# An expert layer on one Trainium2 core: token slots in parts of 64, two experts side by side in a block

## The chip, the core and the metric

The kernel runs on one core of a Trainium2 chip. The core has five engines, each with its own queue of instructions: TensorE (PE; matrix products and transposes, with weight loads shown apart as PEld), VectorE (DVE), ScalarE (ACT), GpSimd (POOL) and SyncE (SP, which here only issues transfers). Sixteen DMA engines move data between the chip's main memory (HBM) and the on-chip memory SBUF; TensorE writes its results into PSUM. The metric is the device time of one execution, in microseconds (us).

## What is computed

The program is one block of a graph network: two graph attention layers and a linear attention over 1250 tokens of 768 features, then a layer of eight experts. The change is in the expert layer alone. Cut to that, the reference is:

```python
def _L0_ffn_ref(x, router_w, w_gate, w_up, w_down, ws_gate, ws_up, ws_down, sg_w, sg_b):
    probs = softmax(x @ router_w)                      # 1250 x 8
    gates, idx = top_k(probs, 2)
    gates = gates / sum(gates)
    dense_g = sum(one_hot(idx, 8) * gates[..., None], axis=-2)
    g = silu(einsum('bsd,edh->bseh', x, w_gate))       # 8 experts, 768 x 768 each
    u = einsum('bsd,edh->bseh', x, w_up)
    expert_out = einsum('bseh,ehd->bsed', g * u, w_down)
    routed = einsum('bse,bsed->bsd', dense_g, expert_out)
    shared = silu(x @ ws_gate) * (x @ ws_up) @ ws_down
    alpha = sigmoid(x @ sg_w + sg_b)
    return alpha * shared + (1 - alpha) * routed
```

Every token goes to two experts, so there are 2500 pairs of token and expert. All numbers are f32.

## The kernel before

Everything up to line 697 (the graph and attention layers) is left alone by the change. The expert layer has four stages.

**Routing (lines 725 to 852).** Tokens are normalised, written to HBM (`xd`) and transposed; the router's scores follow. VectorE then finds the two experts of each token (`hot`), counts the tokens of each expert (`seen`), and lays the experts out one after another in a list of slots. An expert gets as many blocks of 128 slots as its tokens need: `cmp` compares its count with 0, 128, 256, ... (`steps`), `nb` is its number of blocks, `sb` the running sum over the experts. `slot` says in which slot each pair lies; POOL scatters the token numbers into the list `who` in HBM, and SP loads it back as `ids`. `blk` holds the expert of each block (`be`: how many experts end at or before it, from `jb` and `sb`), and in its last column the number of blocks.

**Shared expert (lines 855 to 867).** A dense layer of width 384 on TensorE; routing runs beside it on the other engines. Its weights `wsgu` and its input `xfT` share SBUF with what comes later: pool `wb` (line 870) takes memory that this stage gives back at `sh.close()`, pool `wa` (line 714) has its own and can be filled while the stage runs.

**Expert blocks (lines 872 to 963).** A block is 128 slots of one expert. For each block, POOL gathers the rows of its tokens (`xin`, line 895), TensorE transposes them (`rows`, to `xT`), multiplies with the gate and the up weights (`up`, half of the 768 columns at a time), ScalarE and VectorE make silu(gate) times up (`h`), TensorE transposes that (`hidden`, to `hT`) and multiplies with the down weights (`down`), and the result is written to `ys` in HBM. Three weight tiles of 2304 KB are fetched for each block by SP (`fetch`), at an address that depends on the block's expert; even blocks use the tiles of pool `wa`, odd blocks those of `wb`.

The number of blocks depends on the data. `NSURE` (23) blocks always run, in a pipeline written out by hand: within step j, TensorE does the first half of up(j), the transposes of block j-1's hidden rows, the second half of up(j), the transposes of block j+1's rows, and down(j-1). Gate and up weights of block j+2 are fetched as soon as up(j) has read the tiles, down's of j+1 when down(j-1) has. Blocks beyond 23, up to `NBLK` (27), stand in nested conditions (line 956) and run one step after another.

**Combination (lines 965 to 987).** POOL gathers each token's two rows of `ys` (20 gathers `yg`), TensorE makes the shared expert's last product (`pds`), VectorE adds everything with its factors, and SP and ACT write the output.

A helper's line stands for all its uses: 906 and 907 are the transposes and their copies out of PSUM, 920 the gate and up products, 929 the down products, 901 the weight fetches.

Of the kernel before, what the change touches and what calls it, by code (L numbers as in the profile page):

```python
# [8 lines left out]
F32 = mybir.dt.float32  # L9
# [4 lines left out]
I32 = mybir.dt.int32  # L14
# [5 lines left out]
P = 128  # L20
# [20 lines left out]
NSURE = -(-2 * N // P) + NE // 2 - 1  # L41
NBLK = (2 * N + NE * (P - 1)) // P
# [15 lines left out]
def gps_block(ctx: ExitStack, tc: tile.TileContext, x, src, dst, norm_g, norm_b, W1, a_src1, a_dst1, b1,  # L58
# [643 lines left out]

    fp = ctx.enter_context(tc.tile_pool(name="ffn", bufs=1, reuse_waits="tile"))
# [4 lines left out]
    blk = fp.tile([TP, NBLK + 1], I32, name="blk")  # L708
    ids = fp.tile([P, NBLK], I32, name="ids")
# [4 lines left out]
    wa = ctx.enter_context(tc.tile_pool(name="wa", bufs=1, reuse_waits="tile"))  # L714

# [9 lines left out]
    with tc.tile_pool(name="fln", bufs=2, reuse_waits="tile") as pw, tc.tile_pool(name="flnps", bufs=1, space=PSUM, reuse_waits="tile") as ps:  # L725
# [9 lines left out]
        steps = pw.tile([TP, NE, NT], F32, name="steps", bufs=1)  # L735
        nc.gpsimd.iota(steps, pattern=[[0, NE], [P, NT]], base=0, channel_multiplier=0,
                       allow_small_or_imprecise_dtypes=True)
        jb = pw.tile([TP, NBLK, NE], F32, name="jb", bufs=1)
        nc.gpsimd.iota(jb, pattern=[[1, NBLK], [0, NE]], base=0, channel_multiplier=0,
# [62 lines left out]
        cmp = pw.tile([TP, NE, NT], F32, name="cmp", bufs=1)  # L802
        nc.vector.tensor_tensor(cmp, seen[:, NT, :, None].to_broadcast([TP, NE, NT]), steps, ALU.is_gt)
        nb = pw.tile([TP, NE], F32, name="nb", bufs=1)
        nc.vector.tensor_reduce(nb, cmp, axis=AX.X, op=ALU.add)
        sb = pw.tile([TP, NE + 1], F32, name="sb", bufs=1)
# [4 lines left out]
        nc.vector.scalar_tensor_tensor(first, sb[:, None, 0:NE].to_broadcast(S3), float(P), seen[:, 0:NT, :],  # L811
# [24 lines left out]
        ends = pw.tile([TP, NBLK, NE], F32, name="ends", bufs=1)  # L836
        nc.vector.tensor_tensor(ends, jb, sb[:, None, 1:NE + 1].to_broadcast([TP, NBLK, NE]), ALU.is_ge)
        be = pw.tile([TP, NBLK + 1], F32, name="be", bufs=1)
        nc.vector.tensor_reduce(be[:, 0:NBLK], ends, axis=AX.X, op=ALU.add)
        nc.vector.tensor_scalar(be[:, 0:NBLK], be[:, 0:NBLK], float(NE - 1), None, op0=ALU.min)  # L840
        nc.vector.tensor_copy(be[:, NBLK:NBLK + 1], sb[:, NE:NE + 1])
        nc.vector.tensor_copy(blk, be)

# [28 lines left out]
    with tc.tile_pool(name="fps", bufs=1, space=PSUM, reuse_waits="tile") as ps:  # L872
        n_blk = nc.values_load(blk[0:1, NBLK:NBLK + 1], min_val=0, max_val=NBLK)

        two = range(2)
        ws = [[(wa, wb)[i].tile([P, KD, D], F32, name=f"w{n}{i}") for n in "gud"] for i in two]
# [10 lines left out]
        experts = {}  # L887

        def fetch(j, *parts):

            if j >= NBLK:
                return
            if 0 in parts:
                experts[j] = nc.sync.value_load(blk[0:1, j:j + 1], min_val=0, max_val=NE - 1)
                nc.gpsimd.indirect_dma_start(
                    out=xin[j % 2], out_offset=None, in_=xd,
                    in_offset=bass.IndirectOffsetOnAxis(ap=ids[:, j:j + 1], axis=0),
                    bounds_check=N - 1, oob_is_err=False)
            for p in parts:
                w = (w_gate, w_up, w_down)[p]  # L900
                nc.sync.dma_start(ws[j % 2][p], w[bass.ds(experts[j], 1)].rearrange("o (k p) f -> p (o k) f", p=P))
# [12 lines left out]

        def up(j, s):
            xT, h = xTs[j % 2], hs[j % 2]
            half = slice(s * HALF, (s + 1) * HALF)
            for pt, w in ((pgs[s], ws[j % 2][0]), (pus[s], ws[j % 2][1])):
                for k in range(KD):
                    nc.tensor.matmul(pt[:, :HALF], xT[:, k, :], w[:, k, half], start=(k == 0), stop=(k == KD - 1))  # L920
            nc.scalar.activation(h[:, half], pgs[s][:, :HALF], AF.Sigmoid)  # L921
            nc.vector.tensor_mul(h[:, half], h[:, half], pgs[s][:, :HALF])  # L922
# [92 lines left out]
```

## Time and profile before

| what | us |
|---|---|
| median of 3 runs | 1679.14 (1664.4 to 1679.84) |
| the profiled execution | 1679.8 |
| its span, first to last instruction | 1678.1 |
| before the shared expert and routing, 0 to 896 | 896 |
| routing and shared expert, 896 to 1028.6 | 132.6 |
| 23 blocks of the pipeline, 1028.6 to 1585.7, but for the last one's down | 557.1 |
| that down and the conditional block, 1585.7 to 1622.0 | 36.3 |
| combination, 1622.0 to the end | 56 |

The view of busy slices cuts the span into 40 equal parts, one digit for each: 9 means that the engine was busy 90% of it or more. The view of stretches gives, for a stretch of time, each engine's busy time and number of instructions, then the granted TensorE clock (1.00 is full speed), the share of time that the DMA engines were busy, and GB/s. In the list of groups, a line shows the source line, the engine, what is written from what, shapes, how often, then busy time and the mean duration of one in ns, and the idle time of the engine before them with what ended it. The timeline shows start, length in us, engine, line and how many instructions were merged into the row. An f32 product leaves two records of TensorE, so a block's 36 products are 72 records. Ends of TensorE's records are modelled; their starts are what to read.

### The profile page before, as it was taken

The numbers are of one execution on the slowest core, as the hardware profiler recorded it, in microseconds if no ns is written. First come the engines' busy times: TensorE is split into PE (matmuls) and PEld (weight loads), VectorE is DVE, ScalarE is ACT, GpSimd is POOL, SyncE is SP. The second block draws the span as 40 slices with busy tenths as digits, with TensorE's granted clock in tenths as the row PEclk, the third lists the DMA queues.
The fourth block names the chain that finished last, engine by engine and source line by source line (L and its number), as shares of the span: only waits on it lengthen the run. The fifth ranks groups of instructions, "written<-read, shape, count | busy, mean of one in ns | idle before, by whom it ended". The sixth has DMA issues, their size and how long they took to land. (4 is left out here: it accounts for less than half of the span.)

```text
span 1678.1 us, 15224 instructions
## 1 busy us (share of the span) xinstructions
PE 1587.1 (95%) x5769; PEld 985.6 (59%) x5769; DVE 728.0 (43%) x1342; ACT 369.9 (22%) x635; POOL 142.6 (9%) x175
## 2 busy tenths in 40 slices
PE   6899889999999899999988999999999999999996
PEld 5666544444455599965555855666666666666553
DVE  7888459212443499966787221111111111111116
ACT  3122211111000188830672200101111110111000
POOL 2211000000000000010000051000000000000014
PEclk9999899999999999999997699999999999999998
DMA  7200041002111100021012267988889888888668
GB/s 193 74 1 1 2 139 53 1 0 68 38 38 38 48 31 31 31 73 27 20 44 84 65 114 251 365 324 333 314 304 355 306 309 332 327 313 305 240 225 247
DMA packets 110020, 254.35 MB, mean 152 GB/s; under 512 B 16019, under 2 KB 38676, under 8 KB 109940
## 3 DMA queue, kind: packets, MB, share of 16 engines
q1 hardware_dynamic: 89578, 206.59, 34.4%
q0 software_dynamic: 14704, 36.62, 7.4%
q10 hardware_dynamic: 5658, 10.08, 1.7%
q8 instruction: 50, 0.82, 0.2%
q14 instruction: 30, 0.25, 0.1%
HBM read 234.39 MB, written 18.80 MB: 151 GB/s over the span
## 5 line engine op out<-in xcount | busy, mean ns | idle before, releaser
L920 PE MATMUL pgb<-wg,xT 128*128 128x384 f32 x576 | 194.0, 487 | 2.3 <-ACT xT L907 2.3
L920 PE MATMUL pub<-wu,xT 128*128 128x384 f32 x576 | 193.6, 486 | 0.0
L929 PE MATMUL pdb<-wd,hT 128*128 128x384 f32 x576 | 189.8, 486 | 0.4 <-ACT hT L907 0.4
L532 PE MATMUL pp<-wkv,xnT 128*125 128x512 f32 x360 | 161.6, 598 | 0.1
L920 PEld LDWEIGHTS pub<-wu,xT 128*128 128x128 f32 x576 | 109.4, 190 | 76.3
L614 PE MATMUL pa<-G,u 125*125 125x199 f32 x800 | 140.4, 336 | 11.1 <-DVE h L622 6.0
L920 PEld LDWEIGHTS pgb<-wg,xT 128*128 128x128 f32 x576 | 107.5, 190 | 72.7 <-ACT xT L907 3.0
L929 PEld LDWEIGHTS pdb<-wd,hT 128*128 128x128 f32 x576 | 107.6, 190 | 70.9 <-ACT hT L907 0.7
L614 PEld LDWEIGHTS pa<-G,u 125*125 125x125 f32 x800 | 135.6, 190 | 16.2 <-issue 7.2
L922 DVE TENSOR_TENSOR h<-h,pgb 128x384 f32<-128x384 f32 x48 | 26.6, 554 | 194.8 <-ACT h L921 194.8
L532 PEld LDWEIGHTS pp<-wkv,xnT 128*125 128x125 f32 x360 | 65.9, 190 | 73.7 <-issue 73.3
L931 DVE COPY y<-pdb 128x768 f32<-128x768 f32 x24 | 23.0, 958 | 188.4 <-PE pdb L929 188.4
L411 PE MATMUL ph<-wg,xnT 128*125 128x400 f32 x240 | 101.9, 531 | 2.6 <-PEq L425 2.5
L595 DVE TENSOR_TENSOR ea<-ea,eb 125x625 f32<-125x625 f32 x120 | 93.9, 804 | 14.8 <-ACT eb L594 7.6
L597 DVE SCALAR_TENSOR_TENSOR u<-ea,cntT 125x625 f32<-125x625 f32 x120 | 94.0, 804 | 14.1 <-PE pa L614 8.0
L594 ACT ACTIVATE eb<-r,g_ss 125x625 f32<-125x625 f32 x120 | 95.0, 816 | 20.7 <-DVE ea L595 20.6
L921 ACT ACTIVATE h<-pgb 128x384 f32<-128x384 f32 x48 | 23.5, 490 | 329.6 <-PE pgb L920 329.6
L479 DVE CUSTOM_DVE_ANT_0 junk<-ssb,absent 125x1250 bf16<-125x1250 f32 x60 | 87.7, 1462 | 15.1 <-DMA ssb<-g_srow_d 13.9
L562 PE MATMUL pq<-xnT,wq 128*128 128x500 f32 (+1 forms) x216 | 81.2, 520 | 4.2 <-DMA wq<-in_L_mix_w_qkv_dram 3.7
L923 DVE TENSOR_TENSOR h<-h,pub 128x384 f32<-128x384 f32 x48 | 26.6, 554 | 134.1 <-PE pub L920 134.1
L648 PE MATMUL pu<-wu,xnT 128*125 128x384 f32 x240 | 81.4, 489 | 2.5 <-DVE acc L653 2.5
L575 PE MATMUL pu<-wp,at 128*125 128x384 f32 x240 | 80.5, 488 | 1.4 <-DVE acc L578 1.1
(234 smaller groups left out, 1762.9 us busy)
## 6 DMA issues: line engine op xcount, KB each, us to landing
wg<-in_L_ffn_w_gate_dram SPq DMA_DIRECT2D x25, 2304.0 KB, 8.9
wu<-in_L_ffn_w_up_dram SPq DMA_DIRECT2D x25, 2304.0 KB, 28.7
wd<-in_L_ffn_w_down_dram SPq DMA_DIRECT2D x25, 2304.0 KB
ys<-y ACTq DMA_DIRECT2D x24, 384.0 KB, 7.1
r<-g_rrow_d POOLq DMA_DIRECT2D x12, 610.4 KB, 8.1
wq<-in_L_mix_w_qkv_dram SPq DMA_DIRECT2D x18, 384.0 KB, 3.4
wkv<-in_L_mix_w_qkv_dram SPq DMA_DIRECT2D x6, 768.0 KB
acc<-in_x_dram POOLq DMA_DIRECT2D x10, 375.0 KB, 10.8
```

The source lines that it names most:

```text
L411: nc.tensor.matmul(ph[:, :2 * CG], xnT[:, k, tok], wg[:, k, s * 2 * CG:(s + 1) * 2 * CG], start=(k == 0), stop=(k == KD - 1))
L479: nc.vector.tensor_tensor_reduce(out=junk, in0=self.ssb, in1=absent[:, dt, :], scale=1.0, scalar=-3.0e38, op0=ALU.add, op1=ALU.max, accum_ ...
L532: nc.tensor.matmul(pp, xnT[:, k, tok], wkv[:, k, :, :], start=(k == 0), stop=(k == KD - 1))
L562: nc.tensor.matmul(pq[:, :qw], wq[:, k, :], xnT[:, k, tok], start=(k == 0), stop=(k == KD - 1))
L575: nc.tensor.matmul(pu[:, s, :HALF], at[:, k, i * TP:(i + 1) * TP], wp[:, k, s * HALF:(s + 1) * HALF], start=(k == 0), stop=(k == KD - 1))
L594: nc.scalar.activation(eb, r[:, 1, :], AF.Exp, bias=ss02[:, st, h:h + 1])
L595: nc.vector.tensor_max(ea, ea, eb)
L597: nc.vector.scalar_tensor_tensor(u, ea, 1.0, cntT[:, st, half * W:(half + 1) * W], op0=ALU.min, op1=ALU.mult)
L614: nc.tensor.matmul(pa[i][:, :CO + 1], u[:, i * TP:(i + 1) * TP], G[:, st, h, :CO + 1], start=(st == 0), stop=(st == NT - 1))
L648: nc.tensor.matmul(pu[:, :HALF], xnT[:, k, t * TP:(t + 1) * TP], wus[s][:, k, :], start=(k == 0), stop=(k == KD - 1))
L920: nc.tensor.matmul(pt[:, :HALF], xT[:, k, :], w[:, k, half], start=(k == 0), stop=(k == KD - 1))
L929: nc.tensor.matmul(pd[:, s, :HALF], hT[:, k, :], ws[j % 2][2][:, k, s * HALF:(s + 1) * HALF], start=(k == 0), stop=(k == KD - 1))
```

## The change

Slots are laid out in parts of 64 instead of blocks of 128 (`PART`, `NPART` = 2), and every expert gets at least two parts. A block is still 128 slots, two parts, but each part has its own expert. With the same inputs `NSURE` becomes 22 and `NBLK` 26.

The weights are kept in three rings of two slots (`wg`, `wu`, `wd`). Block j fetches the weights of its second part's expert into slot j % 2. Its first part belongs to the same expert or to the one whose weights block j-1 fetched, and so lies in the one slot or the other: `place` (computed on VectorE, 0 or 1) says in which, and TensorE reads it into a register (`places`). Each product over 128 slots is now two over 64 (`product`): the first part's results go to PSUM partitions 0 to 63, with weights at an address from the register, the second part's to 64 to 127. The two alternate for each of the six pieces of the sum.

Because block j may still read the slot that block j-1 filled, block j+1's weights can only be fetched when block j has read its own: gate's after all of gate(j), up's after up(j), down's after down(j). For this `up` is parted into `gate` and `up`, both halves of gate now come before up, and the row gathers (`gather`) stand apart from the weight fetches. The gate and up rings lie in pool `wa`, down's in `wb`.

```diff
-NSURE = -(-2 * N // P) + NE // 2 - 1
-NBLK = (2 * N + NE * (P - 1)) // P
+PART = 64
+NPART = P // PART
+NBLK = -(-((NE - 2) * NPART - 2 * (-N // PART)) // NPART)
+NSURE = -(-(2 * N + NE * PART // 2) // P)
...
+    place = fp.tile([TP, NBLK, NPART], I32, name="place")
...
+    rings = [wa.tile([P, 2, KD, D], F32, name=f"w{n}") for n in "gu"]
...
-        steps = pw.tile([TP, NE, NT], F32, name="steps", bufs=1)
+        steps = pw.tile([TP, NE, -(-N // PART)], F32, name="steps", bufs=1)
...
         nc.vector.tensor_reduce(nb, cmp, axis=AX.X, op=ALU.add)
+        nc.vector.tensor_scalar(nb, nb, float(NPART), None, op0=ALU.max)
...
-        ends = pw.tile([TP, NBLK, NE], F32, name="ends", bufs=1)
-        nc.vector.tensor_tensor(ends, jb, sb[:, None, 1:NE + 1].to_broadcast([TP, NBLK, NE]), ALU.is_ge)
+        ends = pw.tile([TP, NBLK * NPART, NE], F32, name="ends", bufs=1)
+        nc.vector.tensor_tensor(ends, jb, sb[:, None, 1:NE + 1].to_broadcast([TP, NBLK * NPART, NE]), ALU.is_ge)
+        pe = pw.tile([TP, NBLK, NPART], F32, name="pe", bufs=1)
+        nc.vector.tensor_reduce(pe, ends.rearrange("p (b i) e -> p b i e", i=NPART), axis=AX.X, op=ALU.add)
+        nc.vector.tensor_scalar(pe, pe, float(NE - 1), None, op0=ALU.min)
         be = pw.tile([TP, NBLK + 1], F32, name="be", bufs=1)
-        nc.vector.tensor_reduce(be[:, 0:NBLK], ends, axis=AX.X, op=ALU.add)
-        nc.vector.tensor_scalar(be[:, 0:NBLK], be[:, 0:NBLK], float(NE - 1), None, op0=ALU.min)
+        nc.vector.tensor_copy(be[:, 0:NBLK], pe[:, :, NPART - 1])
         nc.vector.tensor_copy(be[:, NBLK:NBLK + 1], sb[:, NE:NE + 1])
         nc.vector.tensor_copy(blk, be)
+        nc.vector.tensor_tensor(pe, pe, be[:, 0:NBLK, None].to_broadcast([TP, NBLK, NPART]), ALU.is_equal)
+        nc.vector.tensor_tensor(pe, pe, odd.rearrange("p b i -> p (b i)")[:, 0:NBLK, None].to_broadcast([TP, NBLK, NPART]),
+                                ALU.is_equal)
+        nc.vector.tensor_copy(place, pe)
...
-        ws = [[(wa, wb)[i].tile([P, KD, D], F32, name=f"w{n}{i}") for n in "gud"] for i in two]
+        rings.append(wb.tile([P, 2, KD, D], F32, name="wd"))
...
+        def fetch(j, i):
+            if j >= NBLK:
+                return
+            if i == 0:
+                experts[j] = nc.sync.value_load(blk[0:1, j:j + 1], min_val=0, max_val=NE - 1)
+            w = (w_gate, w_up, w_down)[i]
+            nc.sync.dma_start(rings[i][:, j % 2], w[bass.ds(experts[j], 1)].rearrange("o (k p) f -> p (o k) f", p=P))
+
+        def places(j):
+            at = [j % 2] * NPART
+            if j > 0:
+                for i in range(NPART - 1):
+                    at[i] = nc.tensor.value_load(place[0:1, j, i:i + 1], min_val=0, max_val=1)
+            spots[j] = at
+
+        def product(j, i, pt, rows, s):
+            for k in range(KD):
+                for q, at in enumerate(spots[j]):
+                    part = slice(q * PART, (q + 1) * PART)
+                    w = rings[i][:, at] if isinstance(at, int) else rings[i][:, bass.ds(at, 1)].rearrange(
+                        "p o k f -> p (o k) f")
+                    nc.tensor.matmul(pt[part, :HALF], rows[:, k, part], w[:, k, s * HALF:(s + 1) * HALF],
+                                     start=(k == 0), stop=(k == KD - 1))
...
-        fetch(0, 0, 1, 2)
-        fetch(1, 0, 1, 2)
+        for j in two:
+            gather(j)
+            for i in range(2):
+                fetch(j, i)
+            if j == 0:
+                fetch(j, 2)
+        places(0)
         rows(0)
         for j in range(NSURE):
-            up(j, 0)
+            gate(j, 0)
             if j > 0:
                 hidden(j - 1)
-            up(j, 1)
-            if j + 2 < NSURE + 1:
-                fetch(j + 2, 0, 1)
+            gate(j, 1)
+            if j > 0 and j + 1 < NSURE + 1:
+                fetch(j + 1, 0)
+            if j + 1 < NSURE:
+                places(j + 1)
+            for s in two:
+                up(j, s)
+            if j > 0 and j + 1 < NSURE + 1:
+                fetch(j + 1, 1)
+            gather(j + 2) if j + 2 < NSURE + 1 else None
             if j + 1 < NSURE:
                 rows(j + 1)
             if j > 0:
                 down(j - 1)
-                if j + 1 < NSURE + 1:
-                    fetch(j + 1, 2)
+                fetch(j, 2)
         hidden(NSURE - 1)
         down(NSURE - 1)
+        fetch(NSURE, 2)
```

`gate` is the first third of the old `up` (the gate products, sigmoid, and the product with silu's input), the new `up` the rest; the conditional blocks change in the same way and test the number of parts.

## The prediction

> **What bounds the kernel now.** I read the page's busy slices first, then the busy time by stretch, the groups of instructions, and the timeline. In the slices, and in the stretch from 1028.60 us (the first expert block) to 1585.70 (the end of the pipelined blocks), TensorE is busy almost without a break: 556.50 of 557.10 us, at full granted clock. The DMA engines are busy 84% of it, so they have a margin, but not a large one.
>
> ```profile
> PE   6899889999999899999988999999999999999996
> ...
> DMA  7200041002111100021012267988889888888668
> ```
> ```profile
> 1028.60:1585.70 557.10, 556.50 (x1904) 337.55 (x1903) 71.77 (x114) 61.30 (x136) 22.93 (x23) 1.00 0.84 320
> ```
>
> The groups say what fills it: the three expert products. One f32 product of 128x384 leaves two records here.
>
> ```profile
> L920 PE MATMUL pgb<-wg,xT 128*128 128x384 f32 x576 | 194.0, 487 | 2.3 <-ACT xT L907 2.3
> ...
> L929 PE MATMUL pdb<-wd,hT 128*128 128x384 f32 x576 | 189.8, 486 | 0.4 <-ACT hT L907 0.4
> ```
>
> The timeline of one block shows the price of a record (start to start, 12 records from 1079.50 to 1083.37: 322.5 ns) and of a block (1071.10 to 1095.64: 24.54 us). No gap is left: waits of the other engines end inside it, and only the number of TensorE records and their spacing count.
>
> ```profile
> 1071.10 4.03 PE L920 MATMUL pgb<-wg,xT 128*128 128x384 f32 x12
> 1074.97 4.03 PE L920 MATMUL pub<-wu,xT 128*128 128x384 f32 x12
> 1078.84 0.82 PE L906 MATMUL ptr<-ident,h 128*128 128x128 f32 x6
> 1079.50 4.04 PE L920 MATMUL pgb<-wg,xT 128*128 128x384 f32 x12
> 1083.37 4.03 PE L920 MATMUL pub<-wu,xT 128*128 128x384 f32 x12
> 1087.24 0.82 PE L906 MATMUL ptr<-ident,xin 128*128 128x128 f32 x6
> 1087.89 7.91 PE L929 MATMUL pdb<-wd,hT 128*128 128x384 f32 x24
> 1095.64 0.81 PE L920 MATMUL pgb<-wg,xT 128*128 128x384 f32 x2
> ```
>
> The last block runs alone, in the conditional part. The last two down products start 27.13 us apart and each ends by its own 7.9 to 8.0 us, so this block costs 27.1 us. The first gather of results follows at 1626.91.
>
> ```profile
> 1586.94 7.98 PE L929 MATMUL pdb<-wd,hT 128*128 128x384 f32 x24 [0.44 <-ACT hT L907]
> ...
> 1614.07 7.93 PE L929 MATMUL pdb<-wd,hT 128*128 128x384 f32 x24
> ...
> 1626.91 1.28 POOL L970 DMA_INDIRECT yg<-ys,slot  x1 [71.41 <-SPq L954]
> ```
>
> **Part 1: fewer blocks.** The reference, run on its inputs, gives the experts 175, 102, 203, 585, 230, 390, 409 and 406 tokens. In blocks of 128 that is 2+1+2+5+2+4+4+4 = 24, as the 24 writes of ys on the page confirm. In parts of 64, at least two for each expert, it is 3+2+4+10+4+7+7+7 = 44, so 22 blocks. NSURE becomes 22, so no conditional block runs. One pipelined block (24.54) and the lone one (27.1) go: **-51.6 us**.
>
> **Part 2: the products.** A block had 36 products of 128 columns, 72 records by 322.5 ns = 23.2 us. Now it has 72 products of 64 columns, each streaming the same 384 columns: 144 records. Nothing in this trace runs two products side by side on halves of the array, so I bound it: each pair in the time of one (0), or one after the other (+23.2 us a block). No row is near, so pages decide. The Trainium skill, "TensorEngine Tiling (Array Packing)", Key Properties, says that different tiles can load and multiply in parallel. Against it stands "TensorE: Matmul & The Clock Gate", Measured speedup vs the span model: three column tiles gained 2.38, not 3. Taken as throughput, 79% would stretch 23.2 us to 29.4, 22 x 6.2 = +136 us, and the change would lose. But the same section models the span as one product's time plus about 4 ns for each further tile, a latency that a stream doesn't pay again. I take overlap.
>
> It is not quite free. Records start in program order, and the two records of part A precede the two of part B: A1, then A2 with B1, then B2 with the next A1. Two slots a pair, and one slot more at the end of each uninterrupted run. Transposes cut a block into two runs (gate's second half with up; down with the next gate's first half): 2 x 0.3225 x 22 = **+14.2 us** (from 0, if hardware starts pairs together).
>
> **Part 3: switching the array.** Four times a block the array changes between half-width products and full-width transposes. The same page, Key Properties, says that a change of tiling mode drains TensorE. By the rows, a record lasts 486 ns and the next could start after 322, so a drain would show 164 ns, and about 107 more for a weight load no longer hidden (the step of L456's records): 4 x 0.27 x 22 = +24 us. But the trace has such changes, at transposes onto 4 columns, which the compiled program puts into a tile of 32 columns:
>
> ```profile
> 782.21 0.80 PE L456 MATMUL m_row<-ident,g_rc 125*4 125x125 f32 x6 [1.48 <-DVE g_rc L492]
> ...
> 782.85 0.81 PE L648 MATMUL pu<-wu,xnT 128*125 128x384 f32 x2
> ...
> 783.49 0.59 PE L456 MATMUL m_row<-ident,g_rc 125*4 125x125 f32 x4
> ...
> 783.92 3.39 PE L648 MATMUL pu<-wu,xnT 128*125 128x384 f32 x10
> ```
>
> Six records in 0.64 us, two in 0.64, four in 0.43: the plain steps of 107, 320 and 107 ns across three changes. The rows win: 0, with 24 kept for the range.
>
> **Part 4: TensorE's sequencer.** It now reads one register a block and forms an address for each of 36 products. The nearest rows:
>
> ```profile
> L873 PEldq TENSOR_LOAD <-blk x1: 318/318/318, 1589.0 to 1589.0; - x1
> ...
> L901 SPq FUSED_REGOPS  x75: 37/37/48, 974.0 to 1590.0; - x75
> ...
> 954.85 1.37 PE L762 MATMUL pl<-rw,xfT 128*125 128x9 f32 x12
> ```
>
> L762's 12 load-and-multiply pairs step by 103 ns (the transposes behind them start at 956.08) and transposes by 107, so 144 pairs take at most 15.4 us of sequencer; transposes 1.3; the load with its bounds check 0.5 (318, and 159 and 18 on SP); 36 addresses at 37 to 66 ns (SP's operation and its move) 1.3 to 2.4. Sum 19.6 us, under the 24.5 of the array: cost 0. The cover for the load itself: L873's load, behind all 24 records of L929, ran at 1589.0, over 5 us before their last ended (1594.9). Should all 21 loads run in one bunch, 10.5 us less that lead: +5 once. Upper bound, if an address costs more: see the rivals.
>
> **Part 5: fetches.** Weights per block stay three of 2304 KB; DMA traffic falls with the blocks. What changes is when they may start: the other ring slot can still be read by the current block, so gate's slot is free after gate, up's after up, down's after down. SP issues them in just that order, so none blocks one that is ready earlier. Gate's has up (7.74), transposes (about 1) and down (7.74) = 16.5 us; up's and down's about 17.5.
>
> ```profile
> wg<-in_L_ffn_w_gate_dram SPq DMA_DIRECT2D x25, 2304.0 KB, 8.9
> ```
>
> 8.9 us to landing, one at a time, issued about 8 us apart: hidden, with some 7 us to spare; 7.9 MB per 25.2 us is 312 GB/s against the 320 sustained. Without that cover each late us costs 22. The gather of token rows moves behind up on POOL, where nothing queues behind it but the next (23 instructions in 557 us); 1.0 + 7.2 us against a whole block. At the start, down's first fetch waits for the shared stage's memory (near 1028.9) and block 1's gate and up queue behind it on SP: landings near 1038, 1045 and 1053, needs at 1046.8 (gate) and 1055 (up): 0, but gate's margin is 2 us.
>
> **Part 6: routing and memory.** Twice as wide comparisons and seven small operations on VectorE, about 1.5 us; 0.4 before the slot numbers. Block 0's rows land at 1017.7 + 7.2 = 1024.9 and are used at 1028.64, so 3.7 us cover it. The larger iotas run on POOL at 737 us, far ahead. The larger early rings move the shared weights, which now land about 905 and are used at 924.3: 0.
>
> **Part 7: the end.** The unused prefetch of block 22's down weights is now issued at the last down, as ys is written and the gathers (7.7 MB) begin; before, the unused fetches were over. One fetch is worth 8 us of DMA; POOL's 20 issues of 1.57 us already fill 31 of the 50 us left, so part of it hides: **+5 us** (0 to 8).
>
> **Sum.** -51.6 + 14.2 + 5 = -32.4 us against the profiled execution, 1679.8 us (span 1678.1), beside a median of 1679.14: 1647 us.
>
> **Rivals.**
> *Pairs start together* (no stagger): 1633. For it: nothing but that order of starts is my reading.
> *Switches drain* as the page has it: 1647 + 24 = 1671, no change worth the name. Against it: the rows of L456.
> *No overlap*, the slower side: the halves take turns, at L920 and L929's successors. 22 x 23.2 - 51.6 + 5 = +464: 2144 us, DMA share halved. It decides from little: the saving pays for 46.6 / 22 = 2.1 us a block, that is a pair of 0.70 us where full overlap takes 0.645 and turns take 1.29.
> *The sequencer binds*: with 17.2 us of other work a block, break-even (26.7 us) lies at 263 ns an address; at 318, the price of a register load, a block takes 28.6, which gives 1722. Against it: 37 ns on SP.
> *It doesn't do what it says*: a 45th part would bring a 23rd, lone block, 1674; the nearest count is 17 tokens away from a new part.
>
> **How the numbers follow.** Stagger 0.50 (1647), together 0.15 (1633), drains 0.11 (1671), sequencer or poor overlap 0.11 (1690 to 1800), turns 0.10 (2144), late fetches or a 23rd block 0.03. A measurement here can't tell less than 1%, 17 us, from none. Faster: 0.50 + 0.15 and a third of the drains, 0.68; same 0.12; slower 0.20. The range 1620 to 1705 leaves out turns and most of the poor overlap; its low end also takes in the spread of the runs before (1664.4 to 1679.84).
>
> **What would show it.** Right: 22 writes of ys, no product in a conditional block, a block period near 25.2 us, half-width records starting in twos about 320 ns apart. Wrong: starts evenly 320 ns apart (turns), gaps before the transposes (drains), TensorE idle on issue between pairs (sequencer) or on DMA of a ring (fetches); the gathers' landings well above 11.1 us show the end's share.

## The result and the profile after

| | before | after |
|---|---|---|
| median of 20 runs, us | 1675.89 (1662.8 to 1680.91) | 1665.81 (1659.75 to 1670.3) |
| ratio to before, with its 95% interval | | 0.9952 (0.993 to 0.9974) |
| the profiled execution, us | 1679.8 | 1667.31 |
| its span, us | 1678.1 | 1665.6 |

The kernel after is about 0.5% faster: 12.5 us between the two profiled executions, 10 us between the medians, where 32.4 were forecast. The interval lies below 1, but the gain is less than the 1%, 17 us, that the prediction had named as the least that can be told from none. Before's 20 runs lie in two groups with none between, eight from 1662.8 to 1668.5 us and twelve from 1675.6 to 1680.9; its profiled execution is of the slower one, and beside the faster one, which no kept trace shows, the kernel after gains nothing (medians 1664.6 and 1665.8).

The view of stretches (busy time, then granted clock, DMA share, GB/s) shows pipelined blocks with no break, and then, from just behind the last transposes to the end of the last down product, 19.14 us of which TensorE is busy only 10.30, at a clock of 0.73:

```profile
1082.71:1585.70 502.99, 502.69 (x3122) 228.99 (x3118) 64.40 (x101) 53.71 (x120) 17.95 (x18) 1.00 0.87 312
1585.70:1604.84 19.14, 10.30 (x48) 4.54 (x48) 0.00 (x0) 0.32 (x1) 0.00 (x0) 0.73 0.42 145
```

In the groups, the records of down and gate are about as long as before (means of 493 and 489 ns, where 486 and 487 stood), there are 1056 of each tile where 576 were, and down now waits for a transfer:

```profile
L939 PE MATMUL pdb<-wd,hT 128*64 128x384 f32 (+1 forms) x1056 | 177.5, 493 | 9.1 <-DMA wd<-in_L_ffn_w_down_dram 9.1
L939 PE MATMUL pgb<-wg,xT 128*64 128x384 f32 (+1 forms) x1056 | 178.8, 489 | 2.2 <-DMA wg<-in_L_ffn_w_gate_dram 1.9
```

The timeline of one block of the kernel after answers to the block shown of before (start, length, and how many records a row merges):

```profile
1200.59 7.96 PE L939 MATMUL pdb<-wd,hT 128*64 x48
1208.38 4.04 PE L939 MATMUL pgb<-wg,xT 128*64 x24
1212.35 0.88 PE L945 MATMUL ptr<-ident,h 128*128 128x128 f32 x6
1213.16 4.09 PE L939 MATMUL pgb<-wg,xT 128*64 x24
1217.08 7.91 PE L939 MATMUL pub<-wu,xT 128*64 x48
1224.92 0.88 PE L945 MATMUL ptr<-ident,xin 128*128 128x128 f32 x6
1225.72 7.96 PE L939 MATMUL pdb<-wd,hT 128*64 x48
```

48 half-width records take the time of 24 full-width ones: the halves run side by side. The block period is 1225.72 - 1200.59 = 25.13 us, as forecast (25.2). But the 0.6 us over before's 24.54 sit elsewhere than forecast. The run of down and gate's first half has 36 slots, 36 x 0.3225 = 11.61 us, and takes 1212.35 - 1200.59 = 11.76; the six transposes take 1213.16 - 1212.35 = 0.81 where before showed 0.66 (1078.84 to 1079.50). So 0.15 us are lost at each of the four changes between half-width and full-width work, and nothing on a stagger. The starts of single records say the same (start in us, then what the record is; weight loads are left out):

```
1211.929 pgb   1211.934 pgb          two halves, 5 ns apart
1212.352 ptr                         423 ns later, not 322
...
1212.954 ptr                         the last transpose
1213.157 pgb   1213.164 pgb          203 ns later, not 107
1213.530 pgb   1213.536 pgb          373 ns later, then steps of 322
```

Three places lose time. The first is the start of the block stage. TensorE's last `pn` products of attention (some `pm` products still follow), VectorE's first statistics of the norm, the first router transposes and the first row transposes of the kernel after, and the wait of block 1's gate:

```profile
893.15 1.29 PE L669 MATMUL pn<-u,h 125*97 125x312 f32 x4 [0.27 <-DVE u L602]
...
904.71 1.47 DVE L143 BATCH_NORM_STATS2 ln_st<-acc 125x6 f32<-125x384 f32 x3
...
916.12 1.51 PE L769 MATMUL ptf<-ident,xf 125*128 125x125 f32 x6 [12.05 <-DVE xf L764]
...
1038.02 0.85 PE L945 MATMUL ptr<-ident,xin 128*128 128x128 f32 x6
...
1057.53 4.09 PE L939 MATMUL pgb<-wg,xT 128*64 x24 [1.86 <-DMA wg<-in_L_ffn_w_gate_dram]
```

The same places of the kernel before:

```profile
895.12 1.29 PE L664 MATMUL pn<-u,h 125*97 125x312 f32 x4 [0.81 <-DVE u L597]
...
913.18 1.51 PE L758 MATMUL ptf<-ident,xf 125*128 125x125 f32 x6 [2.36 <-DVE xf L753]
...
1028.64 0.82 PE L906 MATMUL ptr<-ident,xin 128*128 128x128 f32 x6
```

The last `pn` products start 2 us earlier than before, and the `pm` products, the last of attention, even end 6.8 us earlier (904.06 against 910.82); yet the first rows are transposed 9.4 us later. All of the norm's statistics now stand behind the last attention products (before, the first came at 871.39), TensorE idles 12.05 us, and its clock comes back later. Two stretches of 20 us show this, of before and then of after (the clock is the last but two):

```profile
940.00:960.00 20.00, 20.00 (x92) 16.67 (x93) 3.05 (x11) 6.43 (x12) 1.06 (x2) 0.64 0.15 38
960.00:980.00 20.00, 20.00 (x67) 11.96 (x66) 11.39 (x57) 3.38 (x6) 5.18 (x5) 1.00 0.24 79
```
```profile
940.00:960.00 20.00, 20.00 (x77) 16.53 (x76) 2.23 (x6) 5.46 (x10) 1.06 (x2) 0.50 0.15 39
960.00:980.00 20.00, 20.00 (x62) 13.47 (x63) 9.14 (x46) 4.10 (x6) 0.00 (x0) 0.72 0.00 1
```

These two traces have no other clock than 0.50 and 1.00, so a mean of 0.64 in the first stretch puts the return of full clock at about 954 us before, and 0.72 in the second puts it at 971 after.

The second and third places are the last down product and the gathers behind it, in the timeline of the kernel after:

```profile
1584.62 20.61 SPq L922 DMA_DIRECT2D wd<-in_L_ffn_w_down_dram  x2
...
1594.54 10.30 PE L939 MATMUL pdb<-wd,hT 128*64 x48 [9.14 <-DMA wd<-in_L_ffn_w_down_dram]
...
1616.63 1.28 POOL L1026 DMA_INDIRECT yg<-ys,slot  x1 [87.97 <-SPq L1004]
```

SP's row merges two fetches: the last block's, issued at 1584.62, and an unused one for block 22 right after the last down. The first is late: down waits 9.14 us and then runs at reduced clock. The second holds up the gathers: they begin at 1616.63, 11.8 us after the last down's end (1604.84), where before they began 4.9 us after it (1622.0 to 1626.91).

The spans, cut at the first row transposes and at the end of the last down product (from the same timelines, for every kernel of this study; "lead-in" runs from the start of the last `pn` products):

| kernel | lead-in | block stage | tail | span |
|---|---|---|---|---|
| before | 133.5 | 593.4 | 56.1 | 1678.1 |
| after | 144.9 | 566.8 | 60.8 | 1665.6 |
| e1, before with padding | 144.8 | 593.3 | 52.8 | 1683.8 |
| e2, after, late tiles moved | 134.1 | 565.6 | 61.1 | 1657.7 |
| e3, after, last fetch earlier | 142.9 | 561.3 | 57.9 | 1656.4 |
| e4, after, first fetches reordered | 150.1 | 565.6 | 62.6 | 1672.8 |
| e6, after, no unused fetch | 140.2 | 564.9 | 54.5 | 1652.6 |
| e7, after, loops swapped | 143.3 | 801.1 | 58.3 | 1897.6 |
| e8, after, fixed slot | 143.2 | 554.0 | 53.3 | 1643.7 |
| e9, after, transposes moved, split | 140.0 | 578.7 | 60.6 | 1673.7 |
| e9b, after, transposes moved | 140.1 | 560.6 | 61.4 | 1658.6 |
| e11, after, parts of 128 | 140.0 | 590.8 | 52.8 | 1675.7 |
| e12, three remedies | 136.8 | 558.2 | 55.2 | 1644.2 |
| e10, three remedies, two changes | 136.8 | 551.3 | 54.2 | 1637.8 |

### The profile page after: what moved, and what is told of

Read it like the earlier page. It is cut to its first block, busy times and chain, and to the rows that moved or that the text cites. A ratio compares the mean times of both kernels' runs of the same rounds, so it can differ in the third digit from the quotient of the medians.

```text
span 1665.6 us, 18775 instructions
## 1 busy us (share of the span) xinstructions
PE 1554.5 (93%) x7185; PEld 884.8 (53%) x7185; DVE 723.7 (43%) x1337; ACT 364.6 (22%) x623; POOL 143.2 (9%) x174
## 5 line engine op out<-in xcount | busy, mean ns | idle before, releaser
L939 PE MATMUL pdb<-wd,hT 128*64 128x384 f32 (+1 forms) x1056 | 177.5, 493 | 9.1 <-DMA wd<-in_L_ffn_w_down_dram 9.1
L939 PE MATMUL pgb<-wg,xT 128*64 128x384 f32 (+1 forms) x1056 | 178.8, 489 | 2.2 <-DMA wg<-in_L_ffn_w_gate_dram 1.9
L939 PE MATMUL pub<-wu,xT 128*64 128x384 f32 (+1 forms) x1056 | 174.0, 486 | 0.0
L939 PEld LDWEIGHTS pdb<-wd,hT 128*64 128x64 f32 x1056 | 75.2, 139 | 100.7 <-issue 97.6
L939 PEld LDWEIGHTS pub<-wu,xT 128*64 128x64 f32 x1056 | 75.9, 137 | 94.3 <-issue 94.3
L939 PEld LDWEIGHTS pgb<-wg,xT 128*64 128x64 f32 x1056 | 74.2, 137 | 92.0 <-issue 90.5
```

What stands on the lines that cost most here:

```text
L939: nc.tensor.matmul(pt[part, :HALF], rows[:, k, part], w[:, k, s * HALF:(s + 1) * HALF], start=(k == 0), stop=(k == KD - 1))
```

## The experiments

### The late start: e1 and e2

Pool `wa` holds four weight tiles of 18 KB a partition now (two slots each of gate and up) where it held three, and everything stacked above it moved up by 18 KB. In the compiled program's memory plan the norm's pool lay at 183 to 201 KB before and lies at 202 to 221 KB after, and so over weights of the attention stage (`wup`, 209 to 224 KB) that its last products read. The first experiment puts that shift alone into the kernel before:

```diff
+    pad = sh.enter_context(tc.tile_pool(name="pad", bufs=1, reuse_waits="tile")).tile([P, KD, D], F32, name="pad")
+    nc.gpsimd.memset(pad[:1, 0, :1], 0.0)
```

> The kernel before, with one unused 18 KB tile ahead of the shared weights, so that these and the pool of the last layer norm lie 18 KB higher, as in the kernel after. Theory (memory): the norm's tiles then lie on memory that the last attention stage still uses, so the norm's statistics on VectorE start behind the last attention products, TensorE stays longer at half clock, and the first expert block starts 7 to 10 us later (first row transposes at about 1037 us instead of 1028.6), total +7 to +10 us on the kernel before. Rival (routing): the late start of the kernel after comes from its wider comparisons and extra small operations on VectorE, which this kernel hasn't: the first transposes stay within 1.5 us of 1028.6 and the total within 3 us of before.

```profile
915.82 1.51 PE L760 MATMUL ptf<-ident,xf 125*128 125x125 f32 x6 [12.05 <-DVE xf L755]
...
1037.68 0.82 PE L908 MATMUL ptr<-ident,xin 128*128 128x128 f32 x6
```

The same wait of 12.05 us to two digits, and the first rows 9.0 us later than in the kernel before, with none of the new routing in it. The median is 1685.48 us beside 1675.75 of before, ratio 1.0061 (1.004 to 1.0082). Memory it is; the wider routing adds nothing that shows. Which tile of the pool brings the wait wasn't tried. The second experiment takes the shift back in the kernel after:

```diff
-    hTs_s = fp.tile([P, nh, N], F32, name="hTs_s")
-    wsd = fp.tile([P, nh, D], F32, name="wsd")
+    late = ctx.enter_context(tc.tile_pool(name="late", bufs=1, side="right", reuse_waits="tile"))
+    hTs_s = late.tile([P, nh, N], F32, name="hTs_s")
+    wsd = late.tile([P, nh, D], F32, name="wsd")
```

> The kernel after, with the shared expert's hidden rows and down weights moved to the other end of memory, so that the pool of the last layer norm lies about where it lay before. Theory (memory): the norm's statistics go back between the attention products, the first row transposes come at about 1028 us instead of 1038.0, total -8 to -10 us on the kernel after, about 1657. Rival (routing): the first transposes stay at 1036 to 1039 and the total within 3 us of the kernel after.

```profile
912.34 1.51 PE L770 MATMUL ptf<-ident,xf 125*128 125x125 f32 x6 [2.84 <-DVE xf L765]
...
1031.05 0.82 PE L946 MATMUL ptr<-ident,xin 128*128 128x128 f32 x6
```

The wait falls to 2.84 us and the lead-in to 134.1, what it was before (133.5). The first rows came at 1031.05, not 1028, since the last `pn` products started 3.8 us later in this execution; the span is 7.9 us below the kernel after, the ratio to before 0.9924 (0.9889 to 0.9958) beside 0.9952, so 5 to 8 us where 8 to 10 were expected. The two intervals overlap, as do those of e3 and e6 with the kernel after's: in these three the lines show the cause, and the times only agree with it. Block 1's gate doesn't wait for its transfer any more either.

### The last fetch: e3

In the last step, the down product of the block before goes ahead of up, so that up covers the fetch:

```diff
+            if j == NSURE - 1:
+                down(j - 1)
+                fetch(j, 2)
             for s in two:
                 up(j, s)
...
-            if j > 0:
+            if 0 < j < NSURE - 1:
                 down(j - 1)
                 fetch(j, 2)
```

> The kernel after, with the last pipelined block's down fetch issued one product stage earlier: in the last step the down product of the block before stands ahead of the last block's up product, so that up covers the fetch. Theory (no cover for the last fetch): the last down's wait of 9.14 us falls to 0 to 1.5 us and its 24 slots take about 7.9 us instead of 10.30, total -8 to -11 us on the kernel after, about 1656. Rival (the end is set by transfers): the first gather of results keeps its time, and the total changes by less than 2 us.

```profile
1578.07 0.37 SPq L922 DMA_DIRECT2D wd<-in_L_ffn_w_down_dram  x1
...
1588.85 9.65 PE L939 MATMUL pdb<-wd,hT 128*64 x48 [1.84 <-DMA wd<-in_L_ffn_w_down_dram]
```

The wait shrinks from 9.14 to 1.84 us; the fetch takes 10.8 us from issue, a little more than up and the transposes cover. The block stage gets 5.5 us shorter, less than the 8 to 11 expected, since the down product still ran at reduced clock (9.65 us), down(20), pulled forward, now waits 0.55 us, and in this execution the first rows waited for their gather, which made the start 0.6 us longer. The span is 9.2 us lower, the ratio to before 0.9926 (0.9888 to 0.9963), some 4 us by medians of ratios. The mechanism holds; the remedy gives back about half of what the late fetch cost.

### Fetches at the start: e4

In the kernel after, block 0's down fetch waits for memory of the shared stage, and block 1's gate and up fetches stand behind it on SP:

```profile
1041.94 0.37 SPq L922 DMA_DIRECT2D wd<-in_L_ffn_w_down_dram  x1
1042.52 0.39 SPq L922 DMA_DIRECT2D wg<-in_L_ffn_w_gate_dram  x1
```

Here it goes behind them:

```diff
         for j in two:
             gather(j)
             for i in range(2):
                 fetch(j, i)
-            if j == 0:
-                fetch(j, 2)
+        fetch(0, 2)
```

> The kernel after, with block 0's down fetch issued behind block 1's gate and up fetches. Theory (one queue, in order): block 1's gate doesn't wait 1.86 us any more, total -1 to -2 us, just at the edge of what five rounds can tell; in the trace the wait of block 1's first gate product is gone and block 0's down product waits for nothing. Rival: the transfers share one rate, and the first gate waits as long, or the down product of block 0 waits instead: total within 0.5 us, or later.

```profile
1033.35 1.85 SPq L922 DMA_DIRECT2D wg<-in_L_ffn_w_gate_dram  x1
...
1037.37 1.07 POOL L910 DMA_INDIRECT xin<-xd,ids  x1 [13.38 <-DMA ids<-who]
...
1044.63 1.51 PE L945 MATMUL ptr<-ident,xin 128*128 128x128 f32 x6 [5.19 <-DMA xin<-xd,ids]
```

The theory's signs came, its gain didn't. Block 1's gate no longer waits for its weights, and neither does block 0's down product, but 4.6 MB of weights are now in flight when the rows of block 0 are gathered: that gather lands 7.3 us after its issue, where the kernel after needed at most 4.3 (1033.76 to 1038.02), and TensorE waits 5.19 us for it. The list of token numbers was also loaded 3.4 us later than in the kernel after, for which this edit gives no reason, so the 7.2 us of span lost aren't all its doing; the ratio to before is 0.9966 (0.9943 to 0.9989), not clear of the kernel after's. The rival was right that the transfers get in one another's way, though it is the gather that pays. That the fetch at the head of the queue had kept the others off the gather fits these lines, but one trace doesn't show it.

### The end: e6

The kernel after without the fetches and the gather for block 22 ahead of the conditional part; a conditional block would fetch its own weights on entry. For one of the fetches and the last one:

```diff
-            if j > 0 and j + 1 < NSURE + 1:
+            if j > 0 and j + 1 < NSURE:
                 fetch(j + 1, 0)
...
-        fetch(NSURE, 2)
...
                 deeper.enter_context(tc.If(n_part > j * NPART))
+                if j == NSURE:
+                    gather(j)
+                    for i in range(3):
+                        fetch(j, i)
```

> The kernel after, without the three fetches and the gather for block 22 ahead of the conditional part; a conditional block would fetch its own weights. Theory (the merge at the end of the conditional part waits for the unused fetch to land): the first gather of results follows the end of the last down product by about 5 us as before, instead of 11.8, the gathers' issue on GpSimd goes back from a median of 1.59 us to about 1.27, and the total falls by 4 to 7 us on the kernel after (1659 to 1662). Rival (the gathers are limited by their own transfers): the first gather comes earlier, but the last adds on VectorE don't, and the total changes by less than 2 us.

```profile
1588.30 9.80 PE L939 MATMUL pdb<-wd,hT 128*64 x48 [9.41 <-DMA wd<-in_L_ffn_w_down_dram]
...
1603.72 1.28 POOL L1029 DMA_INDIRECT yg<-ys,slot  x1 [106.70 <-issue]
```

The first gather comes 5.6 us after the last down's end (1598.10), and the tail falls from 60.8 to 54.5 us: 6.3 us, as the theory has it; the gathers' issue on POOL takes a median of 1.27 us again, where the kernel after took 1.59. The ratio to before is 0.9916 (0.9883 to 0.9949), 6 us below that of the kernel after. (The span fell by 13.0, but 4.7 of that lie in the lead-in, where the clock came back earlier with the same code.)

### Side by side, in which order: e7 and e8

The product's two loops are swapped, so that part A's six pieces precede part B's:

```diff
-            for k in range(KD):
-                for q, at in enumerate(spots[j]):
+            for q, at in enumerate(spots[j]):
+                for k in range(KD):
```

> The kernel after, with the product's two loops swapped: all six pieces of part A, then all six of part B, instead of A and B in turn. Theory (starts are in program order, and a half takes its next record only when its last has run): the twelve records of a part share slots with those of the other part only where one part's run meets the next, so a product of 24 records takes about 22 to 23 slots of 322.5 ns instead of 12: six products a block, +60 to 66 slots, +19.4 to 21.3 us a block and +426 to 468 us in all (2090 to 2135). Rival (the array takes whichever half is free, so order doesn't matter): block period 25.1 us, total as the kernel after, 1666.

Neither: 1899.32 us, in one run. The timeline shows a block of 36.0 us (1231.57 less 1195.57, the row transposes), not 25.1 and not 45:

```profile
1195.57 0.87 PE L945 MATMUL ptr<-ident,xin 128*128 128x128 f32 x6
1196.37 11.03 PE L939 MATMUL pdb<-wd,hT 128*64 x45
...
1231.57 0.88 PE L945 MATMUL ptr<-ident,xin 128*128 128x128 f32 x6
```

The starts of single records within that down product, in us from its first:

```
A   0.001 0.374 0.696 1.019 1.341 1.664 1.986 2.309 2.631 2.954 3.276 3.599
B                                                   2.637 3.011 3.333 3.656 3.978 ...
A'                                                                  5.274 5.647 ...
```

Which half a record belongs to can be told in this block: part A's records, whose address comes from the register, stand in the trace without a shape, part B's with one. B's first record, thirteenth in the program's order, starts 6 ns after A's ninth, ahead of A's last three. So a record may start ahead of earlier ones of the other half, but only a few places ahead: four records out of twelve overlap. A product of 24 takes 2 x 2.63 = 5.27 us, between the 3.87 of full overlap and the 7.1 of strict order. My strict order was wrong, and so was the free choice.

The other experiment fixes part A's ring slot to its own block's, so that TensorE's queue reads no register:

```diff
             at = [j % 2] * NPART
-            if j > 0:
-                for i in range(NPART - 1):
-                    at[i] = nc.tensor.value_load(place[0:1, j, i:i + 1], min_val=0, max_val=1)
```

> The kernel after, with part A's ring slot fixed to that of its own block: no register load and no computed address on TensorE's queue. It leaves out the choice of part A's slot, so that part A of a block with two experts uses the second's weights; fetches may also be released a little earlier. Theory (a change of array mode costs 0.15 us, the queue nothing): block period stays at 25.14 us and the transposes' step at 0.81 us, total within 3 us of the kernel after. Rival (the 0.15 us at each change are addresses that the queue hasn't ready): period 24.54 us, transposes' step 0.66, total -13 us.

```profile
1209.08 0.88 PE L942 MATMUL ptr<-ident,h 128*128 128x128 f32 x6
1209.88 4.09 PE L936 MATMUL pgb<-wg,xT 128*64 128x384 f32 x24
...
1557.18 24.55 SPq L922 DMA_DIRECT2D wd<-in_L_ffn_w_down_dram  x2
...
1582.42 7.96 PE L936 MATMUL pdb<-wd,hT 128*64 128x384 f32 x48 [0.30 <-ACT hT L943]
...
1595.36 1.28 POOL L1023 DMA_INDIRECT yg<-ys,slot  x1 [69.97 <-SPq L1001]
```

The transposes' step is still 0.80 us and the block 25.13 (row transposes 1196.51 to 1221.64): the changes cost what they cost without any address. But the total is 1645.97, ratio 0.9842 (0.9789 to 0.9895), 18 to 20 us below the kernel after, which neither theory had. The lines say why: the last down waits for no transfer and runs at full clock, and the gathers begin 5 us after it. With a fixed slot, a block doesn't read the other one, so the next fetch into it is released a block earlier, the last fetch (at 1557.18 here, 1584.62 in the kernel after) and the unused one among them. What this run prices is the choice of the slot: 9.1 + 2.3 us at the last down and 7.5 in the tail.

### Fewer changes of mode: e9, e9b and e11

Row transposes of block j+1 move right behind the hidden transposes of block j-1, through down's PSUM banks, which are idle then (how the banks are passed is left out):

```diff
...
             if j > 0:
                 hidden(j - 1)
+                if j + 1 < NSURE:
+                    rows(j + 1)
             gate(j, 1)
...
-            if j + 1 < NSURE:
+            if j == 0:
                 rows(j + 1)
```

> The kernel after, with the next block's row transposes moved right behind the hidden transposes of the block before (they go through the down product's idle PSUM banks), from block 2 on: two changes of array mode a block instead of four. Theory (each change costs about 0.15 us): block period 25.14 - 0.30 = 24.84 us, total -6 us on the kernel after for 20 blocks. Rival 1 (one slot more per run of products, as the prediction had it, with the changes free): up, transposes and down become one run, one slot of 0.3225 us less a block, period 24.82, which this can't tell from the theory except by the starts: then twos of records would start 0.32 us apart at a run's end. Rival 2 (copies of the transposes end too late, and TensorE waits): period 25.1 or more, no gain.

This one answered another question. Presumably since transposes and copies share one PSUM tile, the compiled program put a piece of gate between the first three row transposes and the last three, and that piece was one half of a pair. The block had four changes as ever, and part A ran one piece ahead of part B: two slots more, 25.14 + 2 x 0.3225 = 25.79, and the timeline has 25.78 (hidden transposes 1186.46 to 1212.24). Ratio 1.002 (1.0001 to 1.0038): a split pair costs more than the change that was to be saved. The second attempt makes the same move and issues all six transposes ahead of their copies:

```diff
+            if not 1 < j < NSURE:
+                return turned(xTs[j % 2], xin[j % 2])
+            for k in range(KD):
+                nc.tensor.transpose(pd[:, k // 3, k % 3 * P:(k % 3 + 1) * P], xin[j % 2][:, k * P:(k + 1) * P], ident)
+            for i in two:
+                nc.scalar.copy(xTs[j % 2][:, 3 * i:3 * i + 3, :], pd[:, i, :HALF].rearrange("p (k c) -> p k c", k=3))
```

> The kernel after, again with the next block's row transposes behind the hidden transposes of the block before, but now all six issued before their copies, so that no product falls between them: two changes of array mode a block instead of four. Theory (each change costs 0.15 us, 0.66 us for six transposes else): block period 24.84 us in blocks 2 to 21, total -6 us on the kernel after. Rival (copies end too late, TensorE waits for them at the second half of gate or at down): period 25.1 or more, total the same or more.

```profile
1208.58 0.87 PE L945 MATMUL ptr<-ident,h 128*128 128x128 f32 x6
1209.29 0.82 PE L952 MATMUL pdb<-ident,xin 128*128 128x128 f32 x6
1210.04 4.09 PE L939 MATMUL pgb<-wg,xT 128*64 x24
1213.96 7.91 PE L939 MATMUL pub<-wu,xT 128*64 x48
1221.70 7.91 PE L939 MATMUL pdb<-wd,hT 128*64 x48
1229.44 4.04 PE L939 MATMUL pgb<-wg,xT 128*64 x24
1233.41 0.87 PE L945 MATMUL ptr<-ident,h 128*128 128x128 f32 x6
```

1233.41 - 1208.58 = 24.83 us: two changes less, 0.31 us less. Up runs into down without a gap. The median is 1658.25, ratio 0.9909 (0.9885 to 0.9932), about 7 us below the kernel after. And last, the kernel after with full-width parts, no half-width product left:

```diff
-PART = 64
+PART = 128
```

> The kernel after with parts of 128 slots: one expert and one full-width product a block, 24 blocks, all in the pipelined loop, with the kernel after's order of fetches and gathers and its memory. Theory (the 0.60 us a block are the changes of array mode): block period 24.54 us and the transposes' step 0.66 us, the stage of 24 blocks 589 us, so that the total is about 36 us above the kernel after, near 1702. Rival (the 0.60 us come from the kernel after's order of fetches or its memory): period 25.1 us, total near 1716. The start of the block stage is as late as in the kernel after (1034 to 1039 us) in both; the last down's fetch is not held up by part A's slot here, so up to 11 us of that may be missing from the total in both.

```profile
1213.35 0.82 PE L945 MATMUL ptr<-ident,xin 128*128 128x128 f32 x6
1214.01 7.91 PE L939 MATMUL pdb<-wd,hT 128*128 128x384 f32 x24
...
1614.91 7.98 PE L939 MATMUL pdb<-wd,hT 128*128 128x384 f32 x24 [0.44 <-ACT hT L946]
```

Transposes 0.66 us, period 24.54 (down 1189.47 to 1214.01): the whole 0.60 us a block belongs to half-width work beside full-width transposes. The total, 1677.38 in one run, missed the 1702 because this kernel's end has neither the late fetch nor the held-up gathers (tail 52.8 us), and its lead-in was 4.9 us shorter. Beside it the change's real trade is seen: 24 blocks of 24.54 in 590.8 us against 22 of 25.14 in 566.8, of which 13.3 are waits and a slow down product.

### All remedies: e12 and e10

e12 is e2, e3 and e6 in one kernel; e4 is left out. e10 adds the edit of e9b.

> Three remedies together on the kernel after: the shared expert's late tiles at the other end of memory, the last down's fetch one product stage earlier, and no fetches for block 22 ahead of the conditional part. If the three causes are separate their gains add: -5 to -8 for the start, -7 to -9 for the last fetch, -6 for the merge, together -18 to -23 us on the kernel after: 1643 to 1648. If two of them hide one another (the last block's fetch and the end), -11 to -15: 1651 to 1655.

> The three remedies together, and with them two changes of array mode a block instead of four. By the theory -6 us on the kernel with the three remedies alone: 1637 to 1642. By the rival (copies end too late) the same as that kernel or more.

```profile
1575.65 7.96 PE L940 MATMUL pdb<-wd,hT 128*64 x48 [1.84 <-DMA wd<-in_L_ffn_w_down_dram]
...
1589.87 1.28 POOL L1040 DMA_INDIRECT yg<-ys,slot  x1 [110.93 <-PE pds L1048]
```

e12 has a median of 1647.2 us, ratio 0.9855 (0.981 to 0.9901): about 16 us below the kernel after by the ratios, 21.4 by the spans. The gains of e2, e3 and e6, by ratios 5 + 4 + 6, add up, and this interval is clear of the kernel after's. e10 has 1640.7 us, ratio 0.9812 (0.9767 to 0.9856): about 2% below the kernel before, and the fastest of all. Its lines show a last down at full clock and a first gather 6.3 us after it; 1.84 us of wait for the last fetch are left. Behind the same wait e3's last down ran at reduced clock, so the length of the wait alone doesn't decide that.

## Why the prediction was right or wrong

The prediction's 32.4 us became 12.5 because two of its terms were put at nothing. In Part 5, the fetch of the last block's down weights was given a cover that the last block doesn't have: 11.4 us, and 1.9 more at block 1. In Part 6, the shift of memory was costed for one tenant only: 9.4 us until the first rows. The block period, which also had wrong terms, came out right by luck.

**Part 1, fewer blocks: right.** 22 blocks, no conditional one, and -51.6 us for the two saved. e11's 24 blocks in the same program confirm 24.54 for each.

**Part 2, the products: the overlap was right, the stagger wrong.** The halves overlap completely, and pairs start 5 to 7 ns apart, since a record may start ahead of an earlier one of the other half (e7). The rival "pairs start together" had this. The +14.2 us of this step don't exist.

**Part 3, switching the array: wrong.** Here the step that failed is the one where the rows of L456 were taken for 0 against the rule. The change costs 0.15 us (e8, e9b and e11 each leave it or take it away alone), 4 x 0.15 x 22 = +13.2 us. The rule of the Trainium skill, "TensorEngine Tiling (Array Packing)", Key Properties, that a change of mode drains TensorE, fits these changes; the working from it, 0.27 for each change, was nearly twice too much: 423 - 322 = 101 ns are lost at the end of half-width work and 203 - 107 = 96 ns at the end of full-width work, and about 50 more at the first record of the new kind. That the array empties is not shown: the transposes start 423 ns after a record that is modelled to last 486. Why the narrow transposes of L456 showed nothing wasn't tried either. The two errors cancel to 1 us, which is why the block period came out right: the right number for the wrong reason, and only the starts could show it.

**Part 4, the sequencer: right.** Register loads of about 0.3 us lie one to a block and cost nothing; e8 without them has the same block.

**Part 5, fetches: wrong twice, and the larger part of the miss.** It saw that down's slot is now free only after the previous block's down, and gave that fetch 17.5 us of cover from the next block's gate and up. The last block has no next gate and up behind it in that place: 9.14 us of wait, and 2.3 us more for a down product at reduced clock. Only the loop's steady state was costed; in e8, where that fetch is released a block earlier, both losses are gone. The gate's margin of 2 us at the start became a wait of 1.86; that step had named it.

**Part 6, routing and memory: routing right, memory wrong.** "The larger early rings move the shared weights" looked at one tenant of the shifted memory and not at the norm's pool above it. e1 shows the price, 9.0 us to the first rows, of which e2 gets most back. Lead-ins run from 140.0 to 144.9 us with the shift (150.1 in e4, which adds its own wait) and from 133.5 to 136.8 without, so 3 to 11 us a run. The spread comes with the moment at which the clock returns, which the layout doesn't fix: with the shift, runs with full clock by 964 us have 140.0 to 140.2, those that get it at 968 or later 143.2 and more (e3's 142.9 hold a wait of 2.64 us for the gather).

**Part 7, the end: right in size**, +4.7 us in the tail for +5, but by luck, for it is not mainly a collision of transfers: the gathers start 11.8 us after the last down where 4.9 stood before, since the end of the conditional part waits for SP's unused fetch to land. e6 takes 6.3 us out.

In sum against the profiled execution of before: lead-in and start +9.4, block stage -26.5 (forecast -37.4; 11.4 lie at the last down, 1.9 at block 1, and the rest agrees to within 2.5 us), tail +4.7: -12.5 us. Had the last fetch and the memory been costed, the forecast would have been -32.4 + 11.4 + 1.9 + 9.4 = -9.7.

## What to carry to other kernels

When a change makes a buffer's reader run later, follow the released transfer not only in the steady state of the loop but in its first and last turn, where the cover is missing. When a tile grows, list everything that is stacked above it and ask which wait its new neighbour brings; an unrelated stage can pay, and padding the old kernel by the same amount tells it in one run. And a period that comes out right doesn't confirm its terms: look at the starts that each term predicts.

## What the runs showed of the hardware

- Two f32 products of 64 columns each, on the two halves of the array and interleaved in the program, take the time of one of 128: 48 records in 24 slots of 322.5 ns, starts 5 to 7 ns apart.
- Records don't start strictly in program order when they use different halves: a later one overtakes up to three (e7). The Trainium skill, "TensorE: Matmul & The Clock Gate", The mechanism, has products strictly first in, first out; the measured starts decide.
- Each change between half-width products and full-width transposes costs 0.15 us: the block takes 25.13 us with four of them, 24.83 with two (e9b) and 24.54 with none (e11).
- A pair split by other work leaves one part a piece ahead for the rest of the run, and costs that piece's two slots once, at the run's end (e9).
- The same stage with the same code got its full clock back at different moments: 0.72, 0.96 and 0.99 of it in the stretch 960 to 980 us of the kernels after, e3 and e6, whose lead-ins are 144.9, 142.9 and 140.2 us. Differences of that size at this place aren't to be read from one execution.
